# Layer 0 of a four-layer graph network on one core: groups of four samples, three weights side by side, and two levels of Strassen's method

## The chip, the core and the metric

The kernel runs on one core of a Trainium2 chip. The metric is the device time of one execution in microseconds (us). TensorE (PE in the profile) multiplies and writes its sums to PSUM, a memory of eight banks of 512 fp32 columns by 128 partitions. VectorE (DVE), ScalarE (ACT) and GpSimd (POOL) do everything else; PEld is TensorE's loading of the stationary operand, which overlaps with its multiplying. All matmuls here are fp32, and one of them makes two records in the trace; a transpose, which TensorE also makes, has one.

## The reference

128 samples, each of 128 nodes with 512 features, and a 128 x 128 adjacency matrix for each, go through four layers. Every layer is followed by a residual and a normalisation. Only layer 0 is changed:

```python
def _L0_gnn_ref(X, A, Wv, bv, aw, ab, Wk, bk):          # X: (128, 128, 512)
    Xw = X @ Wv + bv
    sj = Xw @ aw[:d, 0]
    si = Xw @ aw[d:, 0]
    e = leaky_relu(sj[:, None, :] + si[:, :, None] + ab[0], negative_slope=0.2)
    alpha_matrix = A * exp(e)
    transition = alpha_matrix / (sum(alpha_matrix, axis=-1, keepdims=True) + 1e-12)
    H, Xk = 0, X
    for k in range(3):
        H = H + Xk @ Wk[k] + bk[k]
        Xk = einsum('bij,bjd->bid', transition, Xk)
    return relu(H)

x = layernorm(x + _L0_gnn_ref(x, adj, ...))             # then layers 1, 2, 3
```

With T for the transition, H = X W0 + T (X W1 + T (X W2)) + biases. The scores sj and si need only X times a vector (Wv times half of aw, made once), so they are dot products of each row of X with two constant rows. The product A * exp(e), which also yields the row sums, is called the masked product below.

## The kernel before

The kernel writes no instruction directly. Each call is recorded with a key (a wished place in TensorE's order), a planner estimates every duration, orders all engines, gives out buffers, and then emits. It knows which operations exclude each other at the memory port that DVE and POOL share:

```python
def shares_port(engine, name, args, kw):
    if engine == POOL:
        return name != "memset"
    views = [a for a in args if isinstance(a, View)]
    sbuf = [a for a in views[1:] if a.tile.kind != "bank" and a.idx.size > 1]
    if engine != DVE or not sbuf:
        return False
    ...
    return len(sbuf) > 1
```

Products are made by Strassen's method (Winograd's form): two samples side by side make the rows of a 2 x 2 block product, which takes seven block products for eight. Four sums of the left side are made by POOL, four of the weights once by DVE:

```python
def strassen(ops, W, nk, nh, take, more=None, flip=False):
    A11, A12, A22, (S1, S2, S3, S4) = ops
    al = bank(); mm(al, A11, B11, True);  take["p1"](al)
    be = bank(); mm(be, S1, T1, True);    take["p5"](be)
    mm(al, S2, T2, False);                take["v"](al)      # sums stay in PSUM and grow
    ga = bank(); mm(ga, A12, B21, True);  take["c11"](ga)
    mm(al, S3, T3, False);                take["c22"](al)
    mm(be, S4, B22, False);               take["c12"](be)
    mm(al, A22, N4, False);               take["c21"](al)
```

(The additions of a transition product to a bank are cut.) Layer 0 handles a pair of samples at a time, with one such product for W2 (256 columns) and one for W1 and W0 together (512 columns). Where an output is X W + T u, the product with T is a further matmul into the same bank. The path of a pair, cut:

```python
def layer0(i0):
    xb = from_dram(x[i0:i0 + U], four, ...)             # X for the transpose
    x0 = load_rows(x[i0:i0 + U]...)                     # X again, kept for the residual
    A = load_adj(i0)
    ...
    for b in range(U):
        dot(s[:, 0, b:b + 1], x0[:, b], wj_b)           # both inputs in SBUF
        dot(s[:, 1, b:b + 1], x0[:, b], wi_b)
    ...
    ops = operands(*blocks(xT))                         # four sums on POOL
    strassen(ops, WT["2"], 2, D // 2, plain_take(*halves(u2)))
    ...
    strassen(ops, WT["10"], 2, D, {
        "p1": lambda p: ac.copy(u1[:, 0], p), "c11": lambda p: add(u1[:, 0], p, u1[:, 0], OP.add),
        ...
    }, {"c11": through(0, u2), "c12": through(0, u1), "c21": through(1, u2)})
    ...
    sp.dma_start(x1d[i0 // U], t)
```

## Time and profile before

| | before |
|---|---|
| time, median of 3 runs | 5660.22 us (5659.11 to 5663.3) |
| span of the profiled run | 5656.1 us |
| TensorE busy | 99% of the span |
| last store of layer 0 | at 1465.4 us |

The lines of the page that matter (busy totals, the 40 slices, the chain that ended last) are shown in the prediction below. How such lines are read: a total gives the busy time of an engine and its share; a slice's digit gives tenths of a fortieth of the span, and 9 means 90% or more; a window row gives a stretch, its length, then the busy time of PE, PEld, DVE, ACT and POOL with their numbers of instructions, and last the granted clock of TensorE as a share of full speed, the DMA share and the GB/s. The start will matter, so here are two such rows of the kernel before:

```profile
20.00:40.00 20.00, 11.46 (x43) 9.68 (x44) 3.04 (x5) 3.48 (x6) 0.00 (x0) 1.00 0.87 185
40.00:60.00 20.00, 19.45 (x63) 12.27 (x62) 16.90 (x35) 4.46 (x13) 8.13 (x10) 1.00 0.06 10
```

From 40 us on TensorE has work (19.45 of 20 us) at full clock. The 1.00 of the first row is not a measurement: the trace of this run has no clock record ahead of 43.0 us, and a stretch without records prints as full speed.

### The profile page before, as it was taken

The page shows a single profiled execution, that of the slowest core. Times are in us where ns is not written, and L with a number is a line of the kernel's source. Part 1 is how long each engine was busy: PE and PEld are TensorE (multiplying, and loading weights), DVE is VectorE, ACT ScalarE, POOL GpSimd, SP SyncE. Part 2 cuts the span into 40 slices and gives each one's busy share as a digit, 9 for nine tenths or more (in the row PEclk, how much of TensorE's full clock was granted, in tenths as well). Part 3 has the DMA queues.
Part 4 walks back from the last instruction along what each step waited for, and adds up shares of the span by engine and source line. Part 5 has one row for each costly group of instructions (what it writes and reads, how often), then busy time and mean ns, then how long its engine had stood idle before and what let it go on. Part 6 is the DMA issues. An engine that isn't in the chain of part 4 may idle for free.

```text
span 5656.1 us, 87535 instructions
## 1 busy us (share of the span) xinstructions
PE 5606.6 (99%) x29151; PEld 4177.8 (74%) x29151; DVE 3680.4 (65%) x7633; ACT 1980.9 (35%) x5057; POOL 2888.2 (51%) x4570
## 2 busy tenths in 40 slices
PE   8999999999999999999999999999999999999999
PEld 5555555555666666666666689999999999999998
DVE  5766665666566666666666667677776777777765
ACT  2322222222333333333333333334333333333433
POOL 2333333333566666666666655555555555555554
PEclk9999999999999999999999999999999999999999
DMA  4433333333343344334434434443344433344432
GB/s 120 117 97 85 95 87 92 90 88 98 99 142 117 116 117 117 115 117 119 117 115 118 127 111 131 131 130 115 122 125 131 131 121 123 121 127 131 131 124 88
DMA packets 718058, 650.22 MB, mean 115 GB/s; under 512 B 259611, under 2 KB 571939, under 8 KB 717606
## 3 DMA queue, kind: packets, MB, share of 16 engines
q1 hardware_dynamic: 714182, 640.15, 38.1%
q10 hardware_dynamic: 3424, 4.46, 0.3%
q8 instruction: 232, 3.80, 0.3%
q14 instruction: 220, 1.80, 0.1%
HBM read 360.20 MB, written 284.16 MB: 114 GB/s over the span
## 4 chain that ended last, share of the span: by engine, by line
PE 90%; DMA 4%; DVE 2%; POOL 2%; SPq 1%; issue 1%; ACT 0%; ACTq 0%; POOLq 0%; DVEq 0%
PE bank L339 90%; DMA four<-x 1%; DMA four<-h 1%; POOL four L339 1%; DVE four L339 1%; SPq L339 1%; DVE col L339 1%; POOL col L339 0%; ACT four L339 0%; DMA four<-in_x_dram 0%; DMA x<-four 0%; DMA four<-S 0%; DMA w<-in_L_gnn_Wk_dram 0%; DMA four<-in_L_gnn_w_dram 0%; DMA sq<-in_adj_dram 0%
## 5 line engine op out<-in xcount | busy, mean ns | idle before, releaser
L339 PE MATMUL bank<-w,four 128*128 128x256 f32 (+1 forms) x14336 | 3999.8, 434 | 20.5 <-DVE four L339 8.2
L339 PEld LDWEIGHTS bank<-w,four 128*128 128x128 f32 x14336 | 2661.6, 190 | 1193.5 <-issue 826.6
L339 DVE TENSOR_TENSOR four<-bank,four 128x256 f32<-128x256 f32 (+1 forms) x1920 | 916.5, 483 | 1329.4 <-PE bank L339 1311.1
L339 ACT COPY four<-bank 128x512 f32<-128x512 f32 (+1 forms) x1286 | 586.7, 458 | 1972.3 <-PE bank L339 1940.2
L339 POOL TENSOR_TENSOR four<-four 128x256 f32<-128x256 f32 (+1 forms) x704 | 547.0, 789 | 943.6 <-PE bank L339 379.7
L339 ACT ACTIVATE four<-four,col,col 128x512 f32<-128x512 f32 (+1 forms) x640 | 562.5, 896 | 876.2 <-POOL col L339 852.3
L339 PE MATMUL bank<-four,w 128*128 128x128 f32 x7168 | 836.1, 276 | 0.6 <-DVE col L339 0.3
L339 PEld LDWEIGHTS bank<-four,w 128*128 128x128 f32 x7168 | 823.7, 192 | 17.3 <-issue 5.9
L339 POOL TENSOR_TENSOR four<-four,four 128x256 f32<-128x256 f32 (+1 forms) x832 | 713.7, 862 | 14.8
L339 POOL TENSOR_SCALAR col<-col 128x1 f32<-128x1 f32 (+1 forms) x704 | 209.6, 301 | 769.4 <-DVE col L339 745.1
L339 DVE BATCH_NORM_STATS2 col<-four 128x6 f32<-128x512 f32 x768 | 527.3, 688 | 92.5 <-ACT four L339 85.5
L339 DVE STREAM_TRANSPOSE four<-four 128x1024 f32<-128x1024 f32 x382 | 471.9, 1235 | 79.3 <-DMA four<-x 53.2
L339 ACT ACTIVATE four<-four,col 128x128 f32<-128x128 f32 x1024 | 395.2, 387 | 228.0 <-DVE col L339 228.0
L339 POOL TENSOR_TENSOR col<-col,neghalf 128x1 f32<-128x1 f32 x640 | 411.4, 646 | 22.2
L339 PE MATMUL bank<-four,sq 128*128 128x512 f32 x768 | 381.7, 592 | 0.2 <-ACT four L339 0.2
L339 POOL TENSOR_TENSOR four<-four,col 128x1024 f32<-128x1024 f32 x128 | 244.9, 1914 | 209.2 <-DVE col L339 209.0
L339 POOL TENSOR_TENSOR four<-four,bo_b 128x512 f32<-128x512 f32 x128 | 162.9, 1279 | 234.8 <-PE bank L339 97.3
L339 PEld LDWEIGHTS bank<-sq,four 128*128 128x128 f32 x2048 | 248.4, 192 | 33.1 <-issue 28.9
L339 DVE SCALAR_TENSOR_TENSOR four<-bank,col,four 128x512 f32<-128x512 f32 x320 | 236.6, 741 | 48.1 <-PE bank L339 41.6
L339 PE MATMUL bank<-four,four 128*64 128x128 f32 (+1 forms) x4096 | 255.0, 278 | 0.0
L339 PEld LDWEIGHTS bank<-four,four 128*64 128x64 f32 (+1 forms) x4096 | 231.3, 163 | 29.8 <-issue 22.4
L339 DVE SCALAR_TENSOR_TENSOR four<-four,four 128x512 f32<-128x512 f32 x256 | 240.3, 955 | 17.6 <-POOL four L339 15.3
(86 smaller groups left out, 3570.2 us busy)
## 6 DMA issues: line engine op xcount, KB each, us to landing
h<-four SPq DMA_DIRECT2D x512, 128.0 KB, 2.4
four<-h SPq DMA_DIRECT2D x128, 512.0 KB, 4.4
S<-four SPq DMA_DIRECT2D x126, 512.0 KB, 3.1
four<-S SPq DMA_DIRECT2D x126, 512.0 KB, 4.5
four<-in_x_dram SPq DMA_DIRECT2D x64, 512.0 KB, 3.8
x1d<-four SPq DMA_DIRECT2D x64, 512.0 KB, 3.1
four<-x1d SPq DMA_DIRECT2D x64, 512.0 KB, 5.7
x2d<-four SPq DMA_DIRECT2D x64, 512.0 KB, 2.8
```

The lines of the kernel that those rows point to most:

```text
L339: call(*map(real, args), **{n: real(a) for n, a in kw.items()})
```

## The change

Its intent is fewer columns for TensorE. The three weights are laid side by side in blocks of 128 rows by 3 x 128 columns, so that all of X [W0 W1 W2] can be made by Strassen's method twice over: four samples make the outer 2 x 2 blocks, and each of the seven outer products is again seven products. That is 49 matmuls of 384 columns per four samples, in place of 28 of 256 and 28 of 512, which are as many columns as 56 of 384. In exchange the outer level's partial sums don't fit PSUM: they are added in SBUF, product by product, mostly by DVE. T (X W2) and the next product then start from X W1 and X W0, which ScalarE copies into a PSUM bank before the matmul adds to it. The diff, cut to its core:

```diff
-BUFS = 17
+BUFS = 12
...
-    slots = {"w28": 3, "w14": 1, "sq": SQS, "col": COLS, "bank": 8, "four": BUFS}
+    slots = {"w7": 7, "out": OUTS, "w28": 0, "w14": 0, "sq": SQS, "col": COLS, "row": ROWS, "bank": 6, "t0": 1, "t1": 1,
+             "four": BUFS}
...
+        for g, half, j in ((0, 0, B11), (1, 0, B21), (0, 1, B12), (1, 1, B22)):
+            ...
+            for m in range(3):
+                ac.copy(to[:, m], stage[m]...)
+            combine(W[j], (ve, po)[half])                                    # inner level, 384 columns
+        for to, a, b in ((T1, B12, B11), (T2, B22, T1), (T3, T2, B11), (N4, B21, T2)):
+            (po if to in (T3, N4) else ve).tensor_tensor(flat[to], flat[a], flat[b], OP.subtract)  # 2688 columns
...
     def layer0(i0):
+        both = [i0 + U * r for r in range(2)]                                # four samples
...
+        for k, (j, take) in enumerate((
+                (B11, fresh(X, bias[:, 0])), (B21, biased_take(C11, X)), (T2, biased_take(X, X)),
+                (T1, fresh(Y, bias[:, 1])), (B22, biased_take(C12, C12)), (T3, biased_take(X, X)),
+                (N4, biased_take(X, X)))):
+            L, S = lefts[k]
+            strassen((L[:, 0, :1], L[:, 0, 1:], L[:, 1, 1:], [S[:, i:i + 1] for i in range(4)]), WT["0"][j], 1, 3 * P, ...)
+            if j in (T1, T3):
+                for b in range(U):
+                    po.tensor_tensor(sides[j == T3 and 2][b], sides[1][b], sides[2][b], OP.add)
...
+            for m in (1, 0):
+                for b in range(U):
+                    p = tile_of(("t0", "t1")[b], D)
+                    ac.copy(p, t[:, m])                                      # seed of the sum
+                    pe.matmul(p, TT[:, b], t[:, m + 1], start=False, stop=True, skip_group_check=True)
```

`biased_take(d, s)` is, for each of the seven outputs of an inner product, a DVE addition of PSUM and SBUF into SBUF over 384 columns; `fresh` splits it, 256 columns copied by ScalarE and 128 added by DVE. The POOL additions over 768 columns (`sides`), which add one outer product's sums to another's, are called side additions below. A PSUM bank into which ScalarE copies a value that a matmul then adds to is called a seeded bank.

The diff does one more thing that the hand-over to layer 1 will need: it puts the preparation of layer 1's weights later, from pair 3 of 64 to the last pairs of layer 0. By the traces their loads are issued from 1293.9 to 1394.6 us, where they were from 100.5 to 243.8.

## The prediction

> **What bounds it now.** I read the page's engine totals first, then its slices, then a table by stage, and last the instructions of one pair of samples in order of time.
>
> From the page of the kernel before:
>
> ```profile
> PE 5606.6 (99%) x29151; PEld 4177.8 (74%) x29151; DVE 3680.4 (65%) x7633; ACT 1980.9 (35%) x5057; POOL 2888.2 (51%) x4570
> PE   8999999999999999999999999999999999999999
> DVE  5766665666566666666666667677776777777765
> POOL 2333333333566666666666655555555555555554
> PE 90%; DMA 4%; DVE 2%; POOL 2%; SPq 1%; issue 1%; ACT 0%; ACTq 0%; POOLq 0%; DVEq 0%
> ```
>
> The first line says that TensorE is busy for all but 50 us of the span. The slices say that this holds in every stage, and the chain that ended last is TensorE's own for nine tenths. Only the first slice has a hole. POOL shows where layer 0 ends: it rises from 3 to 5 in the eleventh slice, at about 1410 us. So layer 0, the stage to be changed, is the first quarter, and there the other engines are still slack. The table by stage (stretch, its length, then busy time of PE, PEld, DVE, ACT and POOL, granted clock, DMA share, GB/s) gives that slack:
>
> ```profile
> 400.00:800.00 400.00, 400.00 (x1207) 222.06 (x1206) 242.47 (x545) 102.57 (x238) 126.94 (x216) 1.00 0.32 90
> ```
>
> TensorE is at 100%, DVE 61%, POOL 32%, ACT 26%, DMA 32%, at full clock. TensorE's own timeline over one pair (start, length, what, number of records; one fp32 matmul makes two records):
>
> ```profile
> 617.08 6.47 PE L339 MATMUL bank<-w,four 128*128 128x256 f32 x28
> 623.38 1.02 PE L339 MATMUL bank<-four,sq 128*128 128x512 f32 x2
> 624.24 0.38 PE L339 MATMUL bank<-ident,col 128*128 128x128 f32 x2
> 624.46 7.03 PE L339 MATMUL bank<-w,four 128*128 128x512 f32 x16
> 631.33 1.02 PE L339 MATMUL bank<-four,sq 128*128 128x512 f32 x2
> ```
>
> Taken from start to start, 14 matmuls of 256 columns take 6.30 us (0.450 each), 8 of 512 take 6.87 us (0.859 each), and the two transposes 0.22 us. The same 28-record group starts again at 639.05, so a pair costs 21.97 us and four samples cost 43.94. Layer 0 is paced by matmul columns and nothing else.
>
> **What the Trainium skill says.** "FP8 and Floating Point Precision", section TensorE Precision Notes, counts four passes for true fp32; "VectorE: DVE Perf Modes", section on the TRN2 errata, gives TensorE 6 cycles plus the columns at 2.4 GHz. Four times 518 cycles is 0.863 us; the trace has 0.859. So columns are what one pays for, and fewer columns should be less time. "SBUF — State Buffer", section Who interferes with whom: a DVE instruction with two SBUF inputs and a GpSimd instruction that reads SBUF exclude each other for the whole instruction, while a DVE instruction with one SBUF input does not contend. The trace agrees: a DVE operation on two SBUF tensors that started beside a POOL addition took 1.21 us, its like 11 us later 0.69. From DVE's timeline, and then POOL's:
>
> ```profile
> 626.60 1.21 DVE L339 SCALAR_TENSOR_TENSOR four<-four,four 128x512 f32<-128x512 f32 x1
> ...
> 637.40 0.69 DVE L339 SCALAR_TENSOR_TENSOR four<-four,four 128x512 f32<-128x512 f32 x1
> ```
>
> ```profile
> 626.42 0.83 POOL L339 TENSOR_TENSOR four<-four 128x256 f32<-128x256 f32 x1 [6.99 <-PE bank L339]
> ```
>
> "PSUM — Partial Sum Buffer", section The four PSUM rules: ScalarE's writes do not touch the bits that make a matmul accumulate, so a seeded bank adds only where an earlier matmul set them. No run yet shows it; the diff runs one matmul over each of the two seeded banks first, so I expect a right result.
>
> **The change, part by part, per four samples (32 groups).**
>
> TensorE. Before: 28 matmuls of 256, 28 of 512 for the weights, 8 of 512 for the transition, 4 transposes: 43.94 us. After: 49 of 384, the same 8, the same 4. A matmul of 384 columns does not occur before; halfway between 0.450 and 0.859 is 0.655, the skill's four times 390 cycles is 0.650, and I take the latter: 49 x 0.650 + 8 x 0.86 + 0.44 = 39.2 us. TensorE saves 4.8 us per group, 153 us in all, 2.7% of the kernel. This would be 5507 us.
>
> DVE. It was 61% of 43.94 = 26.6 us. A 512 addition from PSUM is followed 0.61 us after its start by the next instruction (624.44, 625.05), which is 0.533 for the elements at 0.96 GHz and 0.077 beside; so 0.34 for 256, 0.48 for 384, 0.21 for 128. Out go 6 additions of 256 and 12 of 512, 9.4 us. In come 41 of 384 and 8 of 128, 21.2 us: two levels keep partial sums in SBUF, and nearly every product is added there by DVE. The last step (maximum and residual) now reads PSUM and one SBUF tensor, four times some 0.2 us less. Sum: 26.6 - 9.4 + 21.2 - 0.8 = 37.6 us, 96% of TensorE's 39.2.
>
> POOL. It was 32% of 43.94 = 13.9 us. Eight operand sums of 256 go (5.8 at 0.73). In come 12 of 256 (8.8), 4 of 128 (1.8), 4 of 512 (5.1, at 1.27 as in layer 1) and 4 side additions of 768 (7.3, on the line from 256 to 512). Sum 31.1 us, 79%. These ops read SBUF, and so exclude DVE's 8 dot products (0.65) and 4 masked products (0.25), 6.2 us: together 37.3 us, 95%.
>
> ACT. 11.3 us before; 8 more copies of 512 (the seeds; 0.59 each): 16.0 us, 41%. DMA: x is loaded a third time, 512 KB more per pair, on engines at 32%. Both beside other work.
>
> Start. The first slice's idle 22 us is mostly a wait for x and weights, and the weight bytes stay the same. Before, TensorE could do early products with one weight; now the seven combined weights need 12 ACT copies (0.6 each) and four subtractions over 2688 elements, two of them on DVE (2.9 us each by the rate above), but two blocks can be used before. I put down +4 us. Handing over to layer 1: its weights' preparation (transposes, some 25 us of DVE work) used to lie in layer 0's slack; now it meets a full DVE. +8 us. Layers 1 to 3 keep their instructions, less a buffer move: 0.
>
> Steady state. Three resources now want 39.2, 37.6 and 37.3 us of the same 39.2. The built order of the changed kernel shows how little room there is: TensorE interleaves two of the small Strassen blocks, with six PSUM banks, and the order no longer repeats from group to group as it did. Each accumulation waits for the DVE addition before it; that is hidden while DVE is punctual. DVE is held up by the port: layer 1, with POOL at some 60%, shows the two-SBUF operation at 1.02 us mean instead of 0.69. Twelve such operations per group at some 0.2 us bring DVE to about 40. I choose 40.8 us per group, 1.6 above TensorE's own: 32 x (43.94 - 40.8) = 100 us gained. With +12 at the ends, rounded: 5660 - 100 + 12 = 5572; I lean a little to the planner, which knows of the port and fills gaps: **5568**.
>
> **Rivals.** (a) TensorE stays the bound, and the schedule hides the rest: 5507 plus the ends, about 5520. For it: before, TensorE had no idle time at DVE 61%, and even layers 2 and 3, with DVE at 71%, lose under 1%. Against: no stage ran with DVE above 72%. (b) DVE becomes the bound with port waits as bad as in layer 1 (0.33 us each, 4 us per group, 41.6 us): 75 us gained, 5597. (c) Buffers: 12 general buffers in place of 17, with 14 wanted by one group in turn, so a load may come late; TensorE would wait for DMA. The DMA engines have room, so I give it little; it would add tens of us. (d) Several interleaved waits together hold a group at 44 us: no gain, 5670.
>
> **Range and chances.** A group of 39.5 us gives 5530, one of 42 gives 5610; so 5525 to 5612. The 2% line is at 5547, which needs 40.1 us per group or less with these ends: 0.3. Slower by 2% needs 48 us per group: 0.02. Within 2%: 0.68.
>
> **What the profile will show.** Layer 0's TensorE columns of 384 at 0.65 us; DVE in layer 0 at 88% or more, POOL at 70% or more, ACT some 40%; TensorE at 94 to 98% there, its idle time ended by DVE; layer 0 ending near 1320 us. DVE's dot products should grow from 0.69 toward 0.9 by port waits. The prediction is wrong if the dot products stay at 0.69 and TensorE stays at 99% (then a), if DMA ends TensorE's idle time (c), or if an addition of 384 in a strided result takes clearly more than 0.48.

## The result, and the profile after

The changed kernel gives a right result. Its median is 5614.18 us in four runs (5603.42 to 5615.68), against 5660.51 (5659.11 to 5663.3) for the kernel before on the same chip. The ratio is 0.9913, with a 95% interval of 0.9896 to 0.9931; it is the mean time of one kernel's fast runs over that of the other's fast runs of the same rounds, so not quite the ratio of these medians. All runs were in the fast state. The gain is 0.9%: within 2%, as predicted, and some 46 us of the 92 predicted. The median lies 2 us above the top of the predicted range.

From the page of the changed kernel (totals; slices; the chain that ended last, by engine):

```profile
PE 5500.8 (98%) x28705; PEld 4082.3 (73%) x28705; DVE 4076.2 (73%) x8644; ACT 2130.3 (38%) x5325; POOL 3447.4 (61%) x5076
PE   6999999999999999999999999999999999999999
DVE  6999999999666656666666666767776777777766
POOL 5777777776656666666566555555555555555554
PEclk8999999999999999999999999999999999999999
...
PE 77%; DVE 9%; DMA 6%; POOL 3%; issue 2%; SPq 2%; ACT 1%; DVEq 0%; ACTq 0%; POOLq 0%
```

TensorE's busy time fell by 106 us (from 5606.6), but its idle time rose from 49.5 us to 110.9 (span less busy time). In the second to tenth slices DVE stands at 9 where it stood at 5 to 7 and POOL at 6 to 7 where it stood at 3, and the chain that ended last is now TensorE's for 77% instead of 90%: the shares of DVE, POOL and DMA in it have grown. The first slice is worse than before: 6 instead of 8, at a clock of 8 tenths.

The table by stage, with the stretches that were shown of the kernel before, and 60 to 100 us:

```profile
20.00:40.00 20.00, 9.64 (x40) 8.48 (x40) 3.71 (x8) 3.51 (x6) 0.00 (x0) 0.50 0.86 212
40.00:60.00 20.00, 11.71 (x24) 5.12 (x24) 16.91 (x34) 10.02 (x24) 8.72 (x9) 0.76 0.14 41
60.00:100.00 40.00, 28.37 (x70) 15.02 (x71) 30.94 (x56) 3.93 (x10) 31.31 (x21) 0.80 0.12 33
400.00:800.00 400.00, 390.52 (x1146) 207.46 (x1146) 375.43 (x885) 152.44 (x326) 301.74 (x393) 1.00 0.42 120
```

In the steady stage TensorE went from 100% to 97.6%, DVE from 61 to 94%, POOL from 32 to 75%, ACT from 26 to 38%, DMA from 32 to 42%.

### Where the time went

To add it up I price every TensorE instruction at what it takes back to back (0.11 us for 128 columns, 0.450 for 256, 0.650 for 384, 0.859 for 512) and subtract the price of all that started in a stretch from the stretch's length. What is left is time that TensorE lost, by waits, by small gaps or by a slow clock. This needs no idea of the cause. The price of 384 was taken from the prediction; a run below, in which TensorE hardly waits, has 27 such matmuls in 17.41 us, 0.645 each. Each ledger is that of the one run that was profiled. The prediction's 1.6 us per group is shared out by the products of 384 columns that start in each stretch (those of 0.9, 2.3, 26.8 and 2.0 groups).

| stretch (us) | lost before | lost after | difference | predicted |
|---|---|---|---|---|
| 0 to 100 | 36.2 | 64.0 | +28 | +4, and 1.5 for its groups |
| 100 to 200 | 1.1 | 6.7 | +6 | +4 |
| 200 to 1300 | 6.0 | 58.9 | +53 | +43 |
| 1300 to 1500 | 4.2 | 21.6 | +17 | +8, and 3 for its groups |

The cheaper matmuls were to save 153 us. 153 less these 104 is 49; between 1500 and 1600 another 1.4 go, and the profiled spans differ by 44.4. The rest, some 3 us, is the error of the prices. (In the steady stage they err by more, but in opposite directions: the ledger counts a transpose at half of its 0.11 us and 384 columns at 0.005 too much, some 6 or 7 us each from 200 to 1300. The first is in every row, the second in every row but that of the kernel before, so the changed kernels compare well with each other.) Layers 1 to 3 give and take nothing: the last store of layer 0 is 45 us earlier (1420.3 for 1465.4), the first of layer 1 is 44.7 earlier (1470.6 for 1515.3), and the end 44.4.

So the steady stage lost some 10 us more than was foreseen, and the start five times what was foreseen. First the steady stage. Groups of DVE instructions from 400 to 1200 us of the changed kernel (count, then busy us and mean ns of one, then the idle time ahead of them):

```profile
L362 DVE TENSOR_TENSOR out<-bank,out 128x384 f32<-128x384 f32 x798 | 404.1, 544 | 24.9 <-PE bank L362 16.5 <-POOL out L362 3.6
L362 DVE SCALAR_TENSOR_TENSOR junk<-four,row 128x512 f32<-128x512 f32 x158 | 157.6, 997 | 1.1
...
L362 DVE SCALAR_TENSOR_TENSOR out<-t,four 128x512 f32<-128x512 f32 x79 | 52.4, 672 | 0.1
...
L362 DVE SCALAR_TENSOR_TENSOR sq<-sq,sq 128x128 f32<-128x128 f32 x78 | 33.5, 445 | 1.1 <-ACT sq L362 1.1
```

The first group is the partial sums, half of DVE's time. The second is the dot products, with both inputs in SBUF: 997 ns each. The third has as many columns and nearly as much arithmetic, but one input in PSUM: 672 ns. In the kernel before, the dot products took 673 and 692 ns:

```profile
L339 DVE SCALAR_TENSOR_TENSOR junk<-four,wi_b 128x512 f32<-128x512 f32 x73 | 50.5, 692 | 2.5
...
L339 DVE SCALAR_TENSOR_TENSOR junk<-four,wj_b 128x512 f32<-128x512 f32 x72 | 48.5, 673 | 1.2
```

So 0.31 us of each dot product is not work. The masked products (fourth group) grew in the same way, from 269 to 445 ns. TensorE's timeline shows the effect, a hole in the middle of a row of products that waits for a DVE addition:

```profile
419.56 6.07 PE L362 MATMUL bank<-first,four 128*128 128x384 f32 x18 [0.35 <-ACT out L362]
430.39 2.74 PE L362 MATMUL bank<-first,four 128*128 128x384 f32 x4 [4.76 <-DVE out L362]
```

Then the start, by TensorE's timeline of the first 100 us:

```profile
43.06 1.65 PE L362 MATMUL bank<-first,four 128*128 128x384 f32 x2 [1.70 <-ACT first L362]
45.34 7.25 PE L362 MATMUL bank<-first,four 128*128 128x384 f32 x16 [0.64 <-DVE first L362]
...
60.47 7.48 PE L362 MATMUL bank<-first,four 128*128 128x384 f32 x14 [1.48 <-DVE first L362]
78.27 13.70 PE L362 MATMUL bank<-first,four 128*128 128x384 f32 x34 [10.31 <-DVE first L362]
```

"first" is the block of combined weights. The first product starts at 43.06 us. The kernel before had a first one at 16.06 and a nearly unbroken stream of them from 38.95. At 68 us there is a hole of 10.31 us that ends when DVE has made a combined weight, and DVE's timeline has that instruction twice:

```profile
66.63 3.56 DVE L362 TENSOR_TENSOR first<-first 128x2688 f32<-128x2688 f32 x1
...
75.26 2.95 DVE L362 TENSOR_TENSOR first<-first 128x2688 f32<-128x2688 f32 x1
```

And the products that do run are slow: 7 in 7.48 us (1.07 each), later 17 in 13.70 (0.81 each), where 0.65 is the price. The clock is part of it. The Trainium skill, "TensorE: Matmul & The Clock Gate", Part 1, tells of a gate: half rate after an idle window of about 3.4 us, whole again after a busy one. The trace agrees: the clock records of the changed kernel stand at 0.5 from 14.2 to 48.3 us, from 58.6 to 65.4 and from 72.2 to 82.5, which is 10, 2 and 3 times 3.4 us, and again for 3.4 us from 430.6, right behind the steady stage's hole of 4.76 us. The kernel before must have started at half clock as well: its eight transposes of this stage took 1.97 us, and so did those of the changed kernel at a recorded 0.5. But its records stand at 1.0 from 43.0 to 5634 us. TensorE was busy for 14.2 of the 22.4 us at half rate after 43.0, so the clock added at most half of these, some 7 us. A rough split of the 28 us: the idle times printed in TensorE's timeline from 43.06 to 100 us sum to 17.5, the 10.31 included; the products in between took some 9 us more than their price.

### The profile page after: what moved, and what is told of

Its sections match the earlier page's. It is cut to its first block, busy times and chain, and to the rows that moved or that the text cites. A ratio compares the mean times of both kernels' runs of the same rounds, so it can differ in the third digit from the quotient of the medians.

```text
span 5611.7 us, 88462 instructions
## 1 busy us (share of the span) xinstructions
PE 5500.8 (98%) x28705; PEld 4082.3 (73%) x28705; DVE 4076.2 (73%) x8644; ACT 2130.3 (38%) x5325; POOL 3447.4 (61%) x5076
## 3 DMA queue, kind: packets, MB, share of 16 engines
q1 hardware_dynamic: 731014, 673.45, 40.4%
## 4 chain that ended last, share of the span: by engine, by line
PE 77%; DVE 9%; DMA 6%; POOL 3%; issue 2%; SPq 2%; ACT 1%; DVEq 0%; ACTq 0%; POOLq 0%
PE bank L362 59%; PE t L362 18%; DVE out L362 4%; SPq L362 2%; DVE junk L362 2%; DMA four<-x 2%; POOL four L362 1%; DVE col L362 1%; DMA four<-h 1%; DMA out<-h 1%; DVE four L362 1%; POOL out L362 1%; ACT out L362 1%; DMA four<-in_x_dram 1%; POOL col L362 1%
## 5 line engine op out<-in xcount | busy, mean ns | idle before, releaser
L362 PE MATMUL bank<-first,four 128*128 128x384 f32 (+1 forms) x4904 | 1504.5, 453 | 43.8 <-DVE out L362 18.0
L362 PEld LDWEIGHTS bank<-first,four 128*128 128x128 f32 x4904 | 907.7, 191 | 589.8 <-DVE out L362 136.0
L362 DVE TENSOR_TENSOR out<-bank,out 128x384 f32<-128x384 f32 (+2 forms) x1894 | 931.4, 520 | 268.2 <-PE bank L362 251.3
L362 PE MATMUL bank<-four,four 128*128 128x256 f32 (+2 forms) x2684 | 705.0, 417 | 5.6 <-DVE out L362 2.6
L362 PEld LDWEIGHTS bank<-four,four 128*128 128x128 f32 (+1 forms) x2684 | 401.8, 176 | 242.0 <-issue 198.8
L362 PE MATMUL bank<-first,out 128*128 128x256 f32 x2352 | 532.1, 379 | 0.1
L362 PEld LDWEIGHTS bank<-first,out 128*128 128x128 f32 x2352 | 441.9, 190 | 60.6 <-issue 1.0
L362 PE MATMUL bank<-four,out 128*128 128x256 f32 (+2 forms) x1856 | 482.3, 403 | 3.0 <-DVE out L362 1.4
L362 POOL TENSOR_TENSOR four<-four,four 128x256 f32<-128x256 f32 (+2 forms) x517 | 431.2, 838 | 28.0 <-PE bank L362 14.7
L362 DVE TENSOR_TENSOR four<-bank,four 128x256 f32<-128x256 f32 (+1 forms) x420 | 178.4, 426 | 354.7 <-PE bank L362 345.2
```

The lines of the kernel that those rows point to most:

```text
L362: call(*map(real, args), **{n: real(a) for n, a in kw.items()})
```

## The experiments

My theory of the steady stage was that TensorE waits because DVE is late, and that DVE is late by the exclusion: its twelve two-input operations per group and POOL's reads shut each other out. The rival was DVE's load alone: at 94% it has no slack, whatever the cause of its length. For the start the theory was that the four long subtractions come too late. For the hand-over to layer 1 it was the preparation of layer 1's weights on DVE. The expectations are quoted as they were put down before each run.

Experiments e1 to e6 give wrong results on purpose. They keep the plan of the changed kernel: a hook lets the planner order the original instruction and emits another in its place, so TensorE's order of instructions is the same one. v1 to v7 are right kernels with a new plan each; a few us among them can be luck of the plan. "Group" is the time of four samples, from the stores of layer 0 (20 groups in the middle of it; counted from TensorE's products instead, it agrees to 0.1 us), "lost" as above. All verdicts rest on fast runs, each against the kernel before on the same chip. The dot is the mean time of a dot product.

| kernel | time (us) | ratio, 95% interval | group | dot (ns) | DVE, POOL busy | lost 0–100 | lost 200–1300 | lost 1300–1500 |
|---|---|---|---|---|---|---|---|---|
| before | 5660.51 | 1 | 43.94 | 683 | 61%, 32% | 36.2 | 6.0 | 4.2 |
| after | 5614.18 | 0.9913 (0.9896–0.9931) | 41.13 | 997 | 95%, 76% | 64.0 | 58.9 | 21.6 |
| e1_dots16 | 5574.81 | 0.9856 (0.9828–0.9885) | 40.10 | 448 | 88%, 72% | 63.5 | 31.2 | 18.5 |
| e2_fill | 5563.26 | 0.9836 (0.9807–0.9864) | 39.65 | 680 | 91%, 40% | 60.3 | 22.3 | 19.7 |
| e3_takes256 | 5585.21 | 0.9875 (0.9846–0.9903) | 40.39 | 1008 | 86%, 77% | 64.4 | 38.9 | 15.8 |
| e4_weights64 | 5607.76 | 0.9914 (0.9886–0.9943) | – | – | – | 60.3 | 58.9 | 20.3 |
| e5_one_input | 5574.72 | 0.9851 (0.9822–0.9879) | 39.81 | 673 | 92%, 73% | 63.9 | 28.0 | 18.8 |
| e6_handover | 5609.55, one run | none | – | – | – | 63.9 | 58.5 | 17.4 |
| v1_start | 5621.21 | 0.9928 (0.9905–0.9950) | – | – | – | 75.1 | 55.6 | 23.2 |
| v2_estimates | 5622.49 | 0.9933 (0.9911–0.9956) | – | 1073 | 94%, 74% | 66.6 | 72.5 | 35.6 |
| v3_b5t1r2 | 5578.05 | 0.9852 (0.9836–0.9869) | 39.71 | 677 | 92%, 73% | 63.6 | 28.0 | 25.1 |
| v4_b6t1r1 | 5594.15 | 0.9881 (0.9866–0.9895) | – | 1101, 676 | 96%, 75% | 63.1 | 36.4 | 29.9 |
| v5_b4t2r2 | 5636.28 | 0.9965 (0.9952–0.9978) | – | 682 | 93%, 69% | 62.9 | 73.8 | 34.2 |
| v7_sp | 5576.14 | 0.9858 (0.9841–0.9874) | – | 677 | 92%, 73% | 63.1 | 27.7 | 23.3 |

Busy shares are those from 400 to 1200 us (from 400 to 800 for the kernel before). A dash means that I did not work it out or that it is as in the changed kernel. Of e1 to e6 there are two runs each, of v1 to v7 three to five. The expectations count the steady loss to 1200 us only, which leaves out the first of the last groups: there it is 55.2 us in the changed kernel, 26.1 in e1, 21.9 in e5, 17.1 in v3 and v7, 30.1 in v4, 62.1 in v5 and 68.1 in v2.

### e1: the dot products over 16 columns of 512

The hook, which all of e1 to e6 have, and the edit:

```diff
     def add(self, engine, call, name, args, kw):
+        call = kw.pop("emit", lambda c: c)(call)
...
+    def short(call):
+        return lambda o, u, one, v, **kw: call(o[:, :16], u[:, :16], one, v[:, :16], **kw)
...
-                dot(s[:, 0, b:b + 1], x0[:, b], wj_b)
-                dot(s[:, 1, b:b + 1], x0[:, b], wi_b)
+                dot(s[:, 0, b:b + 1], x0[:, b], wj_b, emit=short)
+                dot(s[:, 1, b:b + 1], x0[:, b], wi_b, emit=short)
```

> Same order of instructions on every engine; only layer 0's eight dot products per group run over 16 columns in place of 512 (wrong scores, so a wrong result on purpose). In the changed kernel one takes 1.0 us on DVE with its wait for the port. Theory (DVE's own load and its waits for the port pace layer 0): DVE loses some 6 us per group, the group of four samples falls from 40.9 us to 39.5 or less, TensorE in 400 to 1200 us rises from 97.6% to over 99%, the kernel takes 5565 to 5580 us in place of 5614. Rival (TensorE is held by its own order of accumulations and six PSUM banks): the group stays within 0.3 us of 40.9 and the kernel above 5600.

The time fell to 5574.81 us, as expected, and the lost time of the steady stage from 58.9 to 31.2; the group, 40.10, did not reach the 39.5 of the theory. The dot product over 16 columns still took 448 ns on average: where the line from 683 ns for 512 columns and 269 for 128 in the kernel before gives some 150 (an estimate). So two thirds of it is waiting, as long a wait as that of the full dot products. But this run takes both work and the blocking of POOL away at once, so it cannot tell load from exclusion.

### e2: POOL writes its sums without reading

```diff
+    def fill(*args):
+        po.tensor_tensor(*args, emit=lambda call: lambda out, u, v, op: nc.gpsimd.memset(out, 0.01))
-            po.tensor_tensor(S1, L[:, :, 1, 0], L[:, :, 1, 1], OP.add)
+            fill(S1, L[:, :, 1, 0], L[:, :, 1, 1], OP.add)
...                                                     (all operand sums and side additions of layer 0)
```

> Same order; POOL's operand sums and side additions of layer 0 become fills that read nothing (wrong result on purpose), so POOL no longer excludes DVE's two-input operations, and DVE's own work stays. If the port is what matters: dot products fall from 1.00 to 0.69 us, masked products from 0.45 to 0.25, DVE from 94% to about 86%, the group from 40.9 to 39.8 us or less, the kernel to some 5580. If DVE's own load matters and the port does not: dot products shorter, but the group above 40.4 us. If POOL itself was a cause through late operand sums, the group falls below what the shorter dot products give, under 39.5.

DVE keeps all its work here, and only what POOL does beside it changes. The dot products of e2 from 400 to 1200 us:

```profile
L363 DVE SCALAR_TENSOR_TENSOR junk<-four,row 128x512 f32<-128x512 f32 x163 | 110.8, 680 | 1.1
```

They are back at 680 ns, the masked products at 280, and a group takes 39.65 us, next to TensorE's own 39.2 of the prediction. 36.6 us of the steady loss are gone. (DVE's share, 91%, fell less than expected, as its groups are shorter too.) This shows that DVE's own work fits into the group. It does not show that reading is the cause, as POOL's work is also shorter (40% busy instead of 76%).

### e3: the partial sums over 256 columns of 384

```diff
+        def two_of_three(call):
+            return lambda d, p, b, op: call(d[:, :2], p[:, :2], b[:, :2], op)
+
+        def add(d, p, b, op):
+            ve.tensor_tensor(d, p, b, op, emit=two_of_three if len(d.shape) == 3 else lambda call: call)
...                                                     (biased_take likewise; results cleared first)
```

> Same order; the 41 additions of a product per group cover 256 of the 384 columns (wrong result on purpose), so DVE loses 41 x 0.13 = 5.5 us per group, and no operation that uses the shared port changes. If DVE's total load matters: group 39.6 us or less, kernel 5570 to 5585. If only the port matters: dot products stay at 1.0 us and the group stays above 40.4 us.

This takes load from DVE and leaves the exclusion: the dots took 1008 ns. DVE fell by 68 us of busy time in the 800 (758.56 to 690.51), more than in any other run, and still the lost time only fell to 38.9 us, a group to 40.39. The expectation of the load theory, 39.6 or less, was missed by far, that of the port theory, above 40.4, by a hair. Load has a part in it, but a small one for its size.

### e5: the dot products with one input

```diff
+    def one_input(call):
+        return lambda o, u, one, v, op0, op1, accum_out: nc.vector.tensor_scalar(
+            o, u, 0.002, None, op0=OP.mult, op1=OP.add, accum_out=accum_out)
...                                                     (the four calls of dot get emit=one_input)
```

> Same order; the eight dot products per group become a scaling with accumulation over the same 512 columns, which takes one SBUF input in place of two (wrong scores on purpose). DVE's own time stays about the same, POOL's work stays the same, only the mutual exclusion of dot products and POOL goes. If the exclusion is what costs: mean of the dot product 0.65 to 0.72 in place of 1.00 us, work lost from 200 to 1200 us falls from 55 to 25 us or less, the kernel takes 5570 to 5585 us. If POOL's lateness itself (its 75% load) was what the fills took away: lost work stays above 40 us, kernel above 5595.

Here the scores are wrong, but the instruction still goes over 512 columns and writes its sum; only the second SBUF input is gone. "SBUF — State Buffer", section Who interferes with whom, says of a DVE instruction with at most one SBUF input that, outside the modes in which DVE uses two ports, it does not contend with GpSimd. The groups and the window of e5:

```profile
L452 DVE TENSOR_SCALAR_CACHE_REDUCE junk<-four 128x512 f32<-128x512 f32 x162 | 109.0, 673 | 1.1
```

```profile
400.00:1200.00 800.00, 795.97 (x2379) 434.53 (x2378) 733.36 (x1844) 316.50 (x685) 580.66 (x811) 1.00 0.44 126
```

And the same window of the changed kernel:

```profile
400.00:1200.00 800.00, 781.39 (x2297) 417.43 (x2296) 758.56 (x1781) 307.91 (x664) 604.15 (x787) 1.00 0.43 122
```

673 ns, no wait left in the dot products. DVE is still 92% busy, and yet TensorE is at 99.5%, a group takes 39.81 us, and 30.9 us of the steady loss are gone. Compare with e3, per group (busy share times group): DVE's busy time was 39.0 us in the changed kernel, 34.9 in e3 and 36.5 in e5. e3 took 4.1 us off DVE and made the group 0.74 us shorter, e5 took off 2.5 and made it 1.32 shorter. A microsecond of DVE's work was worth 0.18, one of its waiting 0.53. So the larger part of the steady loss, some 31 of the 53 us, goes with the exclusion between the dot products and POOL, and not with the load. That a wait costs more than as much work may be because POOL is held up too: its additions of 256 columns took 770 and 776 ns beside these dots and 731 and 730 in v3, where the dots don't exclude it. That second way I only infer. e1 and e3 speak for it: in e1 the dots went on waiting, but held POOL up for so short a time that its additions took 730 ns, and e1 gained as much as e5; in e3 POOL was held as before (770 and 785 ns), and the gain was the least. But e1 took off DVE's work too, so no run parts the wait of DVE from that of POOL.

### e4: the four long weight subtractions over 64 columns of 2688

```diff
-            (po if to in (T3, N4) else ve).tensor_tensor(flat[to], flat[a], flat[b], OP.subtract)
+            (po if to in (T3, N4) else ve).tensor_tensor(flat[to], flat[a], flat[b], OP.subtract, emit=lambda call:
+                lambda o, u, v, op: call(o[:, :64], u[:, :64], v[:, :64], op))
```

> Same order; the four last subtractions that make the combined weights cover 64 of 2688 columns (wrong weights on purpose; filled beforehand). Theory (the start is lost because TensorE waits for the seven combined weights): the 10.3 us hole at 68 to 78 us goes, work lost in the first 100 us falls from 64 to about 50, the kernel takes 5595 to 5602 us. Rival (the start is lost to the transfers of x and weights alone): no change beyond 4 us. Layer 0's group stays at 40.9 us under both.

A miss: the start lost 60.3 us, not the 50 that I had expected, and the 3.7 us gained are within the 4 of the rival, the transfers. But the transfers do not make the hole: in the changed kernel the DMA share is 0.00 from 55 to 85 us. TensorE's timeline still has the hole:

```profile
72.31 14.26 PE L364 MATMUL bank<-first,four 128*128 128x384 f32 x34 [4.98 <-issue]
```

It is 4.98 us long instead of 10.31. The short subtractions still started at 66.00 and 71.99 us in DVE's queue, behind the work of the scores. So the length of the subtractions makes about half of the hole; for the other half I read their place in the queue from this order, and no run has moved them alone. That 5.3 us of hole gave only 3.7 is in part because the first product came 0.9 us later here, at 43.92.

### e6: layer 1's weight subtractions over 32 columns

```diff
-        combine(W)
+        if W is WT.get("w1") or W is WT.get("w2"):
+            short = lambda call: lambda o, u, v, op: call(o[:, :, :32], u[:, :, :32], v[:, :, :32], op)
+            for o, u, v in ((T3, B22, B12), (T1, B12, B11), (T2, B22, T1), (N4, B21, T2)):
+                ve.tensor_tensor(W[:, o], W[:, u], W[:, v], OP.subtract, emit=short)
+        else:
+            combine(W)
```

> Same order; the eight subtractions that make layer 1's combined weights cover 32 columns in place of 512 or 256 (wrong result on purpose), which takes some 9 us of DVE work out of the end of layer 0. If the preparation's DVE work on a full DVE is what the hand-over loses: work lost from 1300 to 1500 us falls from 21.6 to 12 us or less and the kernel to about 5603. If the loss is the last groups' own, or in waits for buffers and transfers: within 4 us of 21.6.

One run took 5609.55 us and was fast. The other took 16767.94 us at a mean granted clock of 0.368; no other kernel here had the like, and there is no ratio. By the trace of the fast run the hand-over lost 17.4 us instead of 21.6, so the rival outcome, within 4 us, was missed by a hair too. These subtractions explain 4 of the 17 us that the hand-over lost more than before. Most of it stays open. The loads of these weights, which the change put into the same stretch, are little of it: by the trace of the changed kernel TensorE and its weight loads waited 1.2 us for them at most.

### v1: weights first in the queues

```diff
-        rank = [o[3] if o[0] == PE or urgent is None else (urgent[k], k) for k, o in enumerate(ops)]
+        rank = [o[3] if o[0] == PE or urgent is None else (-1e9, k) if o[3][0] == -9 else (urgent[k], k) for k, o in enumerate(ops)]
...
-        xbs = [from_dram(x[i:i + U], four, (sp.dma_start,) if i0 else (sp.dma_start, ac.dma_start)) for i in both]
+        xbs = [from_dram(x[i:i + U], four, (sp.dma_start,) if i else (sp.dma_start, ac.dma_start)) for i in both]
```

> A correct kernel. Two changes for the start: the second pair's x is loaded through SP alone, so that ACT's queue is not held before its copies of the weights, and the planner lets the weight preparation go first whenever it is ready. If the start is lost in queues (ACT's copies behind a transfer, DVE's subtractions behind the scores' work): work lost in the first 100 us falls from 64 to 50 to 55 us, kernel 5598 to 5606. If the transfers alone bound it: above 60 us lost. The plan as a whole changes, so a few us either way come from its other parts.

A miss in the other direction: the start lost 75.1 us. The same priority lets the weights' work hold up the score vectors: ScalarE's queue now issued weight transfers from 10.19 to 33.95 us ahead of its first copy, so the products of the score vectors had to wait 24.64 us for ScalarE (to 36.95 us), and the first product came at 55.05 us. So "above 60" came true, but for another reason than the transfers' own time.

### v2: better estimates for the planner

```diff
-        return 67 + n / (1.92 if fast else .96) + (61 * scalars if n > 8 else 0)
+        return 77 + n / (1.92 if fast else .96) + (61 * scalars if n > 8 else 0) + (120 if "accum_out" in kw else 0)
...
-        return 500 + 35 * n if OP.pow in args else 150 + 2.1 * n if n < 800 else 1.82 * n
+        return 500 + 35 * n if OP.pow in args else 190 + 2.1 * n if n < 800 else 1.9 * n
```

> A correct kernel; only the planner's durations change: DVE operations with an accumulated result 120 ns longer, other DVE operations 10 ns, POOL additions 40 ns or 4% longer, as the trace has them. If a good part of the steady loss is the plan being late against the chip (DVE operations that meet a POOL operation which the plan thought was over): dot products below 0.85 us, lost work from 200 to 1200 us 35 to 45 us in place of 55, kernel 5585 to 5600. If the load on DVE and the port leaves no room whatever the order: within 8 us of 55.

The planner knows of the exclusion, and its durations for these operations had come out 10 to 120 ns short. With longer ones the plan was worse than either expectation: dots of 1073 ns, 72.5 us lost in the steady stage. These constants, at least, do not mend the waits.

### v3, v4, v5: the constant rows of the dot products in PSUM

This is e5's lesson as a right kernel: the second input of a dot product is a constant row, and if it lies in PSUM, only one input is in SBUF. A row takes one bank, so banks have to be taken from others: v3 has 5 banks for products, 1 for the seeded sums and 2 rows; v4 has 6, 1 and 1 row; v5 has 4, 2 and 2.

```diff
+SEEDED, KEPT = ('t0',), ('r0', 'r1')                   # v4: ('t0',), ('r0',)   v5: ('t0', 't1'), ('r0', 'r1')
+PSUM = "bank", *SEEDED, *KEPT
...
+        if v.tile.kind in KEPT:
+            u, v = v, u
         ve.scalar_tensor_tensor(junk[:, :n], u, 1.0, v, op0=OP.mult, op1=OP.mult, accum_out=dst)
...
-    wj_b, wi_b = row(), row()
+    wj_b, wi_b = (tile_of(k, D) if k in KEPT else row() for k in ("r0", "r1"))
...
-        pt = bank()
+        pt = dst if dst.tile.kind in KEPT else bank()
...
-                    p = tile_of(("t0", "t1")[b], D)
+                    p = tile_of(SEEDED[b % len(SEEDED)], D)
```

> A correct kernel. Both score rows stay in PSUM through layer 0, so that a dot product has one input in PSUM and one in SBUF and no longer excludes POOL; for the two banks that this takes, the seeded banks go from two to one and the product banks from six to five. If the exclusion is what costs and five banks are enough: dot products 0.65 to 0.75 us, lost work from 200 to 1200 us 20 to 30 us in place of 55, kernel 5570 to 5590. If fewer banks bind in turn: dot products as short, but lost work 40 us or more, kernel above 5595.

v3 gives a right result in 5578.05 us, 0.9852 of the kernel before. Its dot products and its window:

```profile
L363 DVE SCALAR_TENSOR_TENSOR junk<-r,four 128x512 f32<-128x512 f32 x164 | 111.1, 677 | 1.3
```

```profile
400.00:1200.00 800.00, 796.09 (x2383) 434.97 (x2382) 737.63 (x1841) 310.91 (x685) 583.64 (x812) 1.00 0.43 127
```

It is e5 again: 677 ns for 673, TensorE at 99.5%, 28.0 us lost in both. The same cure by another instruction confirms the cause. The lost product bank does no harm that the steady stage shows (17.1 us to 1200, fewer than were expected); the hand-over lost 25.1 us instead of 21.6.

> A correct kernel. Only one of the two score rows in PSUM, one seeded bank, six product banks as in the changed kernel: four of the eight dot products per group no longer exclude POOL. If the exclusion is what costs, about half of the effect: lost work from 200 to 1200 us 30 to 45 us, kernel 5580 to 5600. If one seeded bank in place of two is itself a new limit: lost work 50 us or more here and in the other kernel of this call.

v4 sits in between, as expected of half the cure: 36.4 us lost, 5594.15 us. Its two kinds of dot product took 1101 and 676 ns in the same run, side by side, the plainest sign of what the second SBUF input costs:

```profile
L363 DVE SCALAR_TENSOR_TENSOR junk<-four,row 128x512 f32<-128x512 f32 x80 | 88.1, 1101 | 0.1
...
L363 DVE SCALAR_TENSOR_TENSOR junk<-r,four 128x512 f32<-128x512 f32 x80 | 54.1, 676 | 1.7 <-DMA four<-in_x_dram 1.0
```

> A correct kernel. Both score rows in PSUM and both seeded banks kept, so four product banks are left in place of six. If banks for products are what the two interleaved Strassen blocks need: lost work from 200 to 1200 us 30 us or more in place of 17 with five, kernel above 5590. If the single seeded bank cost more than a product bank (a wait of 5 us on it stands at the end of layer 0): kernel below 5575, lost work below 17 us.

v5 has the dots free (682 ns) and yet is nearly as slow as the kernel before. The waits of TensorE's weight loads from 400 to 1200 us (us in total, times, longest) point to the reason. A late DVE addition ends 119.2 of the 140.5 us for which the trace names an engine:

```profile
PEld bank L363 <- DVE out L363: 119.2, 228, 1.6
```

In v3 that total was 71.5 us in 199 waits, of at most 1.0. I read this as the interleaving of two small Strassen products having no slack with four product banks, so that a product waits for the addition that empties its bank. In these plans five banks were enough and four were not. Not all of it need be the banks: the plan is a new one, its masked products took 818 ns where v3's took 416, and the profiled run is the slowest of the five.

### v7: v3 with one more change of the start

The second pair's transfers are kept off ScalarE's queue, as in v1, without v1's priority.

> A correct kernel: the best so far (five product banks, one seeded, both score rows in PSUM) with the second pair's x loaded through SP alone, so that ACT's queue holds only weights before its copies. If ACT's queue, held for 6 us by that transfer, delayed the weights: lost work in the first 100 us falls from 64 to about 58 us and the kernel from 5578 to some 5572. If the transfers themselves or DVE's queue set the start: 61 us or more lost, kernel within 5 us of 5578, or slower where the new plan is unlucky, as with the first start attempt.

The start lost 63.1 us, as in v3 (63.6): no effect. In the built order ScalarE still issues the four transfers of the first pair ahead of its copies. The time, 5576.14 us, is v3's.

## Why the prediction was right or wrong

**Right: what a matmul costs.** 384 columns were put at 0.650 us; 0.645 was measured where TensorE did not wait. The 153 us are there to be had.

**Right: the loads.** DVE was put at 37.6 us of work and some 2.4 of waits per group; 94% of 41.1 is 38.6, waits counted in. So the sum, 40.0, was 1.4 too high. The rate behind it holds: before the change additions of 512 and 256 columns took 692 and 424 ns, 256 columns in 0.268 us, which is the 0.96 columns per ns of the prediction. POOL was put at 31.1 us, measured 75% of 41.1, 31.0. ACT was put at 16.0, measured 38%, 15.7. An addition of 384 columns into a strided result was put at 0.48 us; three in a row took 1.40, 0.47 each.

**Right: the group.** 40.8 us was chosen, 41.13 measured, and the reason given for it, port waits of the two-input operations that make DVE late, is what e5 and v3 show. The size of one wait was taken too small, 0.2 us against 0.31 for the dots and 0.18 for the masked products, which makes some 0.8 us more of DVE's time per group. Rival (a), TensorE bound at 39.2, was refused for lack of slack in DVE, but e5, with DVE at 92% and no port waits of dots, comes to 39.81: DVE's share alone would have left (a) nearly true. That 40.8 came so close is in part luck: it was chosen and not worked out, and the group came out longer than that although DVE's total came out below its estimate. Rival (c), late loads, does not show: no DMA wait stands among those that end TensorE's idle time from 400 to 1200 us.

**Wrong: the start.** "I put down +4 us"; it was +28, and 6 more to 200 us, of which 5 belong to the 1.6 us per group foreseen. The step counted the work (twelve copies, two subtractions) and not its place: the first product needed the copies and the inner combination, and the stream of products started 4 us later than before, with holes of 17.5 us in it; the outer combination was long and stood behind the scores in DVE's queue, with a hole of 10.31 us; and TensorE was at half clock for 22.4 us after 43.0, for 17.1 of them behind such holes, which no step considered. These 25 us (34 less the 5 and the 4) are more than half of the 46 us by which the median exceeds 5568. Some 10 more are the steady stage's, 6 the hand-over's, and 4 the prediction's step from 5572 to 5568.

**Wrong in size: the hand-over.** "+8 us"; it was +17 by the ledger, 14 without the groups' own 3, and e6 traces 4 to the work named. "Layer 0 ending near 1320 us" failed by 100 us in two ways: the last store moved from 1465.4 to 1420.3, by 45 us and not by some 90, and the prediction had put the end of layer 0 at 1410, the start of the slice in which POOL rises, 55 us ahead of that store. Start and hand-over are the "+12 at the ends", which measured some 43.

**What stays open**: what the hand-over lost beyond those 4 us; what would mend the start, since e4, v1 and v7 each changed something in it and won back 4 us at most; why the last 20 us or so of steady loss remain in e5 and v3; and the one run of e6 at a clock of 0.368.

The best right kernels are v3 and v7, at 5578.05 and 5576.14 us, 1.4 to 1.5% faster than the kernel before and some 0.6% faster than the changed one.

## What to carry to other kernels

When a change moves work to DVE and POOL together, count the instructions of DVE with two SBUF inputs beside POOL's reads, and rather than trimming DVE's work put one of the two inputs in PSUM if it is a constant: here that was worth some 31 us, for two PSUM banks, one taken from the products and one from the seeded sums. Price the start on its own, in the order of the queues and not as a sum of work, because a bound that wants its operands earlier pays there what it saves later. And when an accumulation is emptied by a busy engine, check how many banks stand between: five held here, and a plan with four did not.

## What the Trainium skill lacked or had wrong

- "SBUF — State Buffer", section Who interferes with whom, has the rule of the exclusion right (673 and 677 ns with one SBUF input, 997 with two), but no size for this pairing. Beside a POOL that was 76% busy a two-input operation of 512 columns waited 0.31 us on average, one of 128 columns 0.18, and one of 16 columns still took 448 ns.
- "PSUM — Partial Sum Buffer", its summary of rules for kernel authors, says of a sum seeded by DVE or ACT that the seed must be 0. The section The four PSUM rules on the same page is the more exact: a seed counts where an earlier matmul left the bit set, and 0 is only the seed that is safe either way. Here ScalarE seeds two banks with values other than 0, 8 times per four samples, after one matmul over each bank, and the result is right.
